# Turning bias vectors on TensorE, earlier residual rows and an earlier flip of h in a two-layer graph transformer

## The chip, the cores and the metric

The kernel runs on one core of a Trainium2 chip. The metric is the device time in microseconds of one execution; the time of a kernel is the median over its runs. A profile is taken of one further execution, and its instructions are what the views below are made of. The engines are called PE (TensorE, matmuls and transposes), DVE (VectorE), ACT (ScalarE), POOL (GpSimd) and SP (SyncE, which here only issues DMAs). Each runs its own instructions in the order in which the program emitted them.

## The reference

Two identical layers of a transformer over a graph of N = 2708 nodes with 512 features, 8 heads of 64, and a hidden width of 2048. All is float32.

```
mask = adj + eye
q, k, v = (h @ Wq.T + bq), (h @ Wk.T + bk), (h @ Wv.T + bv)     # 8 heads of 64
scores = q k^T / 8, set to -1e9 where mask == 0
ctx  = softmax(scores) @ v
h1   = layer_norm(h + ctx @ Wo.T + bo) * ln1_g + ln1_b
out  = layer_norm(h1 + relu(h1 @ W1.T + b1) @ W2.T + b2) * ln2_g + ln2_b
```

`adj` is a sparse symmetric 0/1 matrix; the kernel keeps lists of fewer than 24 neighbours a node.

## The kernel before

The nodes are worked on in 22 tiles of 128 (the last one holds 20). Because the graph is sparse, attention is done by edges: for each tile the rows of K and V of the listed neighbours are gathered from a table in DRAM (`kv_d`) and weighed on DVE and ACT. The schedule is written out by hand: the order of instructions in the program is their order on each engine.

**Stage one, keys and lists (`first`, L871).** For each of the 22 tiles, PE projects k and v (`project`, L575), ACT copies them out, POOL adds the bias row bk (L917), and ACT's queue stores the rows in `kv_d`. Beside it, `lists(t)` reads two halves of 128 rows of `adj` (SP, L691), POOL adds the diagonal (L694), ACT codes them (L700), and DVE finds the neighbours by MAX8 (L705). `counted` and `ranked` then sort the nodes by their number of neighbours; two matmuls (L788, L795) use the result.

**Stage two, queries (`first_queries`, L944).** 22 more projections; DVE evicts each with its bias (`evicted`, L951; the last, short tile also needs L597), SP stores pairs of tiles in `q_d` (`written`, L960 and L964). After the third, `last_keys` finishes `kv_d` and attention may begin. The tiles of attention come in the order of `blocks` (L1522), which begins with tiles of few neighbours. The first three tiles of attention make their own queries (`own_rows`, `turned_own`, `own_query`); all others gather theirs from `q_d` once all queries are stored (`asked`, L1073). `beside_queries(t)` is called after each query: it loads weights, settles biases (`settle`, L1276), and calls `advance`.

**Attention runs ahead by credit.** `attend` (L1527) is a generator of chunks of at most two neighbours. `advance(more)` (L1584) adds to a credit of at most 1.5 and emits chunks while it is positive; a chunk of two costs 1, of one 0.5, an empty step 0.2. `through(k)` (L1594) emits whatever is missing for a block. A finished tile leaves its context `cx` in `got`.

**Feed-forward, per block of two tiles.** `attended` (L1366) transposes cx on PE (`flip`, L1233, the tile `tp`), fetches the residual rows (`residuals`, L1357; in layer 0 a gather on POOL, in layer 1 a load on SP), projects by Wo (`o`), adds, and normalizes to h (`norm`, L1218, with the power of -1/2 on POOL, L1227). `turned` (L1389) flips h to hT. `feed_forward` (L1398) does 16 steps f: four matmuls into `pf` per step and pass (L1445), ACT's relu to `ft` (L1456), and the second matmul into `a` (L1418) three steps later. The main loop (L1635) places, after each step f of block k, what else is done there: the next block's residuals, flips and projection, chunks of attention by the tables `PACES` (block 0) and `PACE`, and in layer 0 the next layer's keys and values (`keys_values`, L1485).

**Biases.** `lined` (L560) copies bk and bq, which lie in DRAM as 128 x 4 columns, into a DRAM row by one DMA whose pieces are single elements; `row_of` (L567) reads this row into all partitions. `column` (L603) reads bv, b2 and the next layer's bo, which lie in DRAM as rows, into 128 x 4 columns, again element by element. `settle` negates b2 and bo and adds pairs of rows.

Of the kernel before, what the change touches and what calls it, by code (L numbers as in the profile page):

```python
# [479 lines left out]
def by_edges(ctx: ExitStack, tc: tile.TileContext, x, xT, adj, layers, out, redo):  # L480
# [35 lines left out]
    lines = []  # L516
# [43 lines left out]
    def lined(w, name, by):  # L560

        line = dram.tile([1, DM], F32, name=f"{name}_d{len(lines)}")
        lines.append(line)
        by.dma_start(out=line.rearrange("o (c p) -> p (o c)", p=P), in_=w[name])
        return line
# [37 lines left out]
    def column(w, name):  # L603
        t = small.tile([P, NC], F32, tag=name, name=name, bufs=1)
        nc.sync.dma_start(out=t, in_=w[name].rearrange("o (c p) -> p (o c)", p=P))
        return t
# [264 lines left out]
    def first(w, meanwhile):  # L871
# [29 lines left out]
        short = [lined(w, name, nc.scalar) for name in ("bk", "bq")]  # L901
        finish(halves)
        wv = matrix(w, "Wv", "wv")
        bk = row_of(short[0], "bk")
# [3 lines left out]
        for t in range(NT):  # L908
            r = size(t)
            if t == NT - 1:  # L910
                parts = placing[0](*counts)
            xs = tokens(t, 0)
            kv = wts.tile([P, 2 * DM], F32, tag=f"w2_{5 + t % 3}", name="kvs")
            k = project(xs, r, wk, "k")
            if t < NT - 1:
                nc.scalar.copy(kv[:r, :DM], k[:r])
                nc.gpsimd.tensor_tensor(kv[:r, :DM], kv[:r, :DM], bk[:r], ALU.add)  # L917
            v = project(xs, r, wv, "v", other=True)
            nc.scalar.copy(kv[:r, DM:], v[:r])
            if before:  # L920
                nc.scalar.dma_start(**before)
            before = dict(out=kv_d[0][t * P : t * P + r, :], in_=kv[:r])
            if t == 0:
                finish(load())
            while done < min(NT, 1 + LEAD * t):
                lists(done)
                done += 1
                if done == NT:
                    counts = counted()
            meanwhile(t)  # L930
            if t == QT:
                wq = matrix(w, "Wq", "wq", nc.gpsimd)
            if t == NT - 4:
                bq = row_of(short[1], "bq", DK**-0.5)
# [9 lines left out]
    def first_queries(bq, wq, parts, inverted, pa, tokens, last_keys, meanwhile):  # L944
# [21 lines left out]
        for t in range(NT):  # L966
# [25 lines left out]
            if t == OWN:  # L992
                zTs = [turned_own(g, xr) for g, xr in zip(blocks[0], xrs)]
                for g, zT in zip(blocks[0], zTs):
                    own_query(g, zT, to[g], bq, wq)
                    advance(0.5)
            if t == OWN + 5:
                own_query(order[2], turned_own(order[2], xrs[2]), to[order[2]], bq, wq)
# [247 lines left out]
    class Layer:  # L1246
# [5 lines left out]
        def load_first(self):  # L1252
            w = self.w
            self.wo = matrix(w, "Wo", "wo", nc.gpsimd if self.n == 0 else None)
            self.bv = column(w, "bv")
            if self.n == 0:
                self.bo = row(w, "bo")
            self.g1 = row(w, "ln1_g")
            self.nb2 = column(w, "b2")
            self.unsettled = [self.nb2]  # L1260
# [15 lines left out]
        def settle(self):  # L1276
            for t in self.unsettled:
                if isinstance(t, tuple):
                    nc.vector.tensor_tensor(t[0], t[0], t[1], ALU.add)
                else:  # L1280
                    nc.vector.tensor_scalar(t, t, -1.0, None, ALU.mult)
# [21 lines left out]
        def load_next(self):  # L1303

            nxt = layers[self.n + 1]
            self.short = [lined(nxt, name, nc.sync) for name in ("bk", "bq")]
            self.nbo = column(nxt, "bo")
            self.unsettled.append(self.nbo)

        def preloaded(self, tiles, temp):  # L1310
# [10 lines left out]
            return list(zip(tiles, places))  # L1321

# [250 lines left out]
    def settled():  # L1573

        held = small.tile([P, 1], F32, tag="held", name="held", bufs=1)
        nc.vector.tensor_reduce(held, flags, AX.X, ALU.min)
        pr = ps.tile([P, DM], F32, tag="g", name="pr")
        nc.tensor.matmul(pr[:1, :1], ones[:, :1], held, start=True, stop=True)
        nc.vector.tensor_scalar(redo, pr[:1, :1], P - 0.5, None, ALU.is_lt)
        return nc.values_load(redo[0:1, 0:1], min_val=0, max_val=1)  # L1580
# [29 lines left out]
    def beside_queries(t):  # L1610
# [9 lines left out]
        if t > OWN:  # L1620
            advance(0.65)
        if t == NT - 6:
            through(0)
            early[0] = now.attended(blocks[0], got)
            next(early[0])
        if t == NT - 5:
            for _ in blocks[0]:
                next(early[0])

# [5 lines left out]
    for n in range(NL):  # L1635
        last = n == NL - 1
        nxt = None if last else Layer(n + 1, layers[n + 1])
        if n > 0:
# [6 lines left out]
            both = dn.tile([P, 2, NC, P], F32, tag="hT", name="zTs", bufs=1)  # L1645
            for i, g in enumerate(order[8:10]):
                nc.sync.dma_start(out=both[:, i], in_=zT_d[n][g])
                pool.append((g, both[:, i]))
# [6 lines left out]
            for i, _ in enumerate(streamed):  # L1655
                if i == 4:
                    now.stores = nc.sync
                if len(got) < 2 or i < 4:
# [4 lines left out]
            streamed = now.queries(order[16 : 2 * AHEAD])  # L1663
            next(streamed)
            for _ in blocks[0]:
                next(early[n])
            for i, _ in enumerate(streamed):
                if i < 3:
                    advance(0.6)
            now.apart = False  # L1670
            now.load_w2(NFC // 2 - 1)
        *_, hs = early[n]
        hT = now.turned(blocks[0], hs)
        projecting = xbs = None
        for k, block in enumerate(blocks):
# [4 lines left out]
            for f, zs in enumerate(now.feed_forward(block, hs, hT)):  # L1680
# [24 lines left out]
                if last and not more and f == 8:  # L1705
                    checked()
                if last and not more and f == 14:
                    again = settled()
                if not more and f == 0:
                    finish(ahead)  # L1710
                if not last:
# [6 lines left out]
                    if (k, f) == (1, 0):  # L1718
                        now.settle()
                    if (k, f) == (NB - 1, 0):  # L1720
                        places.clear()
                        now.wq = matrix(nxt.w, "Wq", "wq")
                    if (k, f) == (1, 0):
                        now.bk = row_of(now.short[0], "bk")
                        nxt.bq = row_of(now.short[1], "bq", DK**-0.5)
# [83 lines left out]
```

## Time and profile before

| | |
|---|---|
| runs | 1880.89, 1882.51, 1883.33 us; median 1882.51 |
| profiled execution | 1880.68 us, of which the span from first to last instruction is 1879.0 us |
| mean granted clock of PE | 0.993 |
| busy | PE 1833.0 us, DVE 1373.1, ACT 944.1, POOL 781.8 |
| DMA | 368.00 MB, mean 196 GB/s |

Busy time is an instruction's own time; a line of the timeline gives the start, the duration, the engine, the program's line, the operation, out<-in with shapes, how many were merged, and in brackets the idle time of the engine before it with the instruction that ended it. "issue" there means that nothing the profile shows was waited for. The list of waits gives for an engine and line what it waited for: total microseconds, times, the longest. A row of the windows gives from:to, length, busy time and instructions of PE, weight loads, DVE, ACT and POOL, then the granted clock, the busy share of the DMA engines and the rate in GB/s. A name such as `L585` is a line of the kernel; all projections share that line.

### The profile page before, as it was taken

How to read it: one execution, taken by the hardware profiler on the slowest of the kernel's cores; microseconds unless marked ns; L12 is line 12 of the kernel's file. 1: busy time of each engine (PE TensorE's matmuls, PEld its weight loads, DVE VectorE, ACT ScalarE, POOL GpSimd, SP SyncE). 2: the span in 40 equal slices, each digit the busy share in tenths (PEclk: the TensorE clock that was granted, in tenths of full speed). 3: DMA queues.
4: the chain of work that ended last, by engine and by line, in shares of the span. 5: the costliest groups of instructions: out<-in, count | busy, mean ns of one | idle time of the engine just before them, and what ended most of it. 6: DMA issues, size and time to landing. Idle time of an engine off the chain costs nothing.

```text
span 1879.0 us, 20852 instructions
## 1 busy us (share of the span) xinstructions
PE 1833.0 (98%) x6140; PEld 1087.8 (58%) x6140; DVE 1373.1 (73%) x2143; ACT 944.1 (50%) x3261; POOL 781.8 (42%) x745
## 2 busy tenths in 40 slices
PE   7999978999999999999999999999999999999997
PEld 3444435656656566565665544566666666666664
DVE  3987847876867777677774237878988998899842
ACT  3771426555545555555553214556746575657531
POOL 3233745544444444353530113526543554455302
PEclk9999998999999999999999999999999999999999
DMA  9998958555465554554531477736545664545300
GB/s 279 367 340 258 379 182 308 185 174 173 153 212 174 185 184 141 196 192 137 191 124 69 144 256 291 288 133 217 220 157 196 215 236 140 216 169 203 128 1 20
DMA packets 133933, 368.00 MB, mean 196 GB/s; under 512 B 18518, under 2 KB 36774, under 8 KB 133808
## 3 DMA queue, kind: packets, MB, share of 16 engines
q0 software_dynamic: 70608, 252.12, 38.7%
q1 hardware_dynamic: 53106, 93.63, 14.5%
q10 hardware_dynamic: 10094, 20.81, 3.0%
q8 instruction: 50, 0.82, 0.2%
q14 instruction: 75, 0.61, 0.1%
HBM read 315.84 MB, written 50.68 MB: 195 GB/s over the span
## 4 chain that ended last, share of the span: by engine, by line
PE 88%; DVE 4%; DMA 4%; issue 2%; ACT 1%; POOL 1%; ACTq 0%; POOLq 0%; SPq 0%; DVEq 0%
PE pf L1445 29%; PE a L1418 29%; PE v L585 8%; PE k L585 8%; PE o L585 7%; PE q L585 4%; PE tp L1237 2%; DVE kv L1101 1%; DMA kv<-kv_d,listed 1%; DVE sc L1107 1%; DMA bq_d<-in_bq 1%; DMA q_d<-qs 1%; ACT kv L1127 1%; PE a L1433 1%; DMA xb<-in_x,ident_i 0%
## 5 line engine op out<-in xcount | busy, mean ns | idle before, releaser
L1445 PE MATMUL pf<-hT,w 128*128 128x256 f32 (+1 forms) x2816 | 634.7, 373 | 18.7 <-ACT ft L1456 15.6
L1445 PEld LDWEIGHTS pf<-hT,w 128*128 128x128 f32 x2816 | 520.0, 191 | 192.9 <-issue 104.3
L1418 PE MATMUL a<-w,ft 128*128 128x512 f32 x1312 | 611.1, 592 | 0.0
L1064 POOL DMA_INDIRECT kv<-kv_d,listed x420 | 502.2, 1196 | 256.5 <-issue 113.1
L1456 ACT ACTIVATE ft<-pf,b 128x256 f32<-128x256 f32 (+1 forms) x336 | 154.3, 462 | 415.4 <-PE pf L1445 411.6
L1418 PEld LDWEIGHTS a<-w,ft 128*128 128x128 f32 x1312 | 246.9, 190 | 187.5 <-issue 166.6
L1227 POOL TENSOR_TENSOR rd<-va,mhalf 128x1 f32<-128x1 f32 (+1 forms) x88 | 81.8, 929 | 584.7 <-DVE va L1225 584.7
L1127 ACT ACTIVATE kv<-kv,p 128x64 f32<-128x64 f32 x1232 | 311.0, 334 | 5.0
L1101 DVE TENSOR_TENSOR kv<-kv,q 128x1024 f32<-128x1024 f32 (+1 forms) x222 | 256.9, 1157 | 21.5 <-DMA q<-q_d,ident_i 15.7
L1107 DVE TENSOR_REDUCE sc<-kv 128x16 f32<-128x1024 f32 (+1 forms) x222 | 258.0, 1162 | 7.6
L1140 DVE TENSOR_TENSOR acc<-acc,kv 128x1024 f32<-128x1024 f32 (+2 forms) x178 | 205.4, 1154 | 78.4 <-ACT kv L1127 66.8
L1120 ACT ACTIVATE p<-sc,listed 128x8 f32<-128x8 f32 x420 | 104.7, 300 | 144.6 <-DVE sc L1107 103.8
L1133 DVE TENSOR_TENSOR kv<-kv,p 128x512 f32<-128x512 f32 (+1 forms) x178 | 122.6, 689 | 47.0 <-ACT p L1120 28.6
L585 PE MATMUL o<-wo,cT 128*128 128x512 f32 x336 | 149.6, 598 | 0.0
L585 PEld LDWEIGHTS o<-wo,cT 128*128 128x128 f32 x336 | 64.2, 192 | 81.6 <-issue 76.2
L705 DVE MAX8 tops<-code 128x8 f32<-128x247 f32 (+2 forms) x242 | 78.5, 400 | 35.9 <-ACT code L700 35.9
L1231 DVE SCALAR_TENSOR_TENSOR h<-h,rd,ln_b 128x512 f32<-128x512 f32 (+1 forms) x88 | 66.5, 755 | 39.9 <-POOL rd L1227 39.9
L1171 ACT ACTIVATE cx<-acc,su 128x64 f32<-128x64 f32 (+1 forms) x352 | 88.2, 333 | 13.4 <-DVE su L1163 7.7
L1380 DVE TENSOR_TENSOR h<-o,xb 128x512 f32<-128x512 f32 (+1 forms) x44 | 30.2, 687 | 86.7 <-PE o L585 53.2
L1127 ACT ACTIVATE acc<-kv,p 128x64 f32<-128x64 f32 (+1 forms) x352 | 88.9, 335 | 1.4
L585 PE MATMUL k<-wk,xg 128*128 128x512 f32 x168 | 77.4, 604 | 11.6 <-DMA wk<-in_Wk 11.6
L700 ACT ACTIVATE code<-aj 128x1354 bf16<-128x1354 int32 (+1 forms) x44 | 72.8, 1720 | 19.0 <-POOL aj L694 13.8
(168 smaller groups left out, 1522.7 us busy)
## 6 DMA issues: line engine op xcount, KB each, us to landing
aj<-in_adj SPq DMA_DIRECT2D x42, 677.0 KB
kv_d<-kvs ACTq DMA_DIRECT2D x21, 512.0 KB
xg<-in_xT SPq DMA_DIRECT2D x19, 512.0 KB
w<-in_W SPq DMA_DIRECT2D x16, 512.0 KB
kv<-kv_d,listed POOLq DMA_INDIRECT x420
zT_d<-zT SPq DMA_DIRECT2D x22, 256.0 KB
xb_d<-h SPq DMA_DIRECT2D x21, 256.0 KB
q<-q_d SPq DMA_DIRECT2D x21, 256.0 KB
```

Of the source, the lines that this page charges most:

```text
L585: nc.tensor.matmul(o[:r], xs(c), wm[:, c, :], start=(c == 0), stop=(c == NC - 1))
L1064: return nc.gpsimd.indirect_dma_start(out=to, out_offset=None, in_=table[:, :], in_offset=bass.IndirectOffsetOnAxis(ap=s, axis=0), bounds_ ...
L1101: nc.vector.tensor_tensor(kv[:r, :c, :DM], kv[:r, :c, :DM], self.q[:r].unsqueeze(1).to_broadcast([r, c, DM]), ALU.mult,)
L1107: nc.vector.tensor_reduce(self.sc[:r, s0 : s0 + c, :], kv[:r, :c, :DM].rearrange("p s (h d) -> p s h d", d=DK), AX.X, ALU.add,)
L1120: nc.scalar.activation(p[:r, s, :], self.sc[:r, s, :], AF.Exp, bias=minus[:r, g, s : s + 1])
L1127: nc.scalar.activation(to[:, i, hd], kv[:r, i, DM + h * DK : DM + (h + 1) * DK], AF.Copy, scale=p[:r, s0 + i, h : h + 1],)
L1133: nc.vector.tensor_tensor(to[:, 0, :].rearrange("p (h d) -> p h d", d=DK), kv[:r, 0, DM:].rearrange("p (h d) -> p h d", d=DK), p[:r, s0, : ...
L1140: nc.vector.tensor_tensor(self.acc[:r, :c, :], self.acc[:r, :c, :], kv[:r, :c, DM:], ALU.add)
L1171: nc.scalar.activation(cx[:r, hd], self.acc[:r, 0, hd], AF.Copy, scale=self.su[:r, h : h + 1])
L1418: nc.tensor.matmul(a[:r], fts[f][:, c0 : c0 + r], self.w2[f // 2][:, f % 2, :], start=(f == 0), stop=(f == NFC - 1),)
L1445: nc.tensor.matmul(pf[:, :w], self.w1[f // 2][:, c, f % 2 * P : f % 2 * P + P], hT[:, c, :w], start=(c == 0), stop=(c == NC - 1),)
L1456: nc.scalar.activation(ft[:, :w], pf[:, :w], AF.Relu, bias=self.b1[:, f : f + 1])
```

## The change

Three things are changed together.

1. *Biases.* bk and bq are loaded as 128 x 4 columns (`given_columns`, SP), transposed on PE into one PSUM tile, copied by ACT, and stored as two DRAM rows of 4 x 128 (`lined`). In layer 0 this stands behind k of tile 0, and tile 0's bias is added at the end of its turn. bv, b2 and bo are loaded as 4 x 128 rows (`raw_columns`), and `settle` transposes them on PE and takes the sign on DVE. The next layer's bk and bq are loaded in `load_next`, turned at (k, f) = (1, 0) and read back at (1, 2).
2. *Residual rows and attention in layer 0.* The first block's own queries come one query later than their flips (`OWN + 1`), and `advance` starts one query later; the residual rows are gathered at query NT - 10 instead of NT - 6, the flips of cx come at NT - 7, the projection by Wo at NT - 6.
3. *h before the last query.* In both layers h of the first block is turned in front of the last query instead of behind it. In layer 1 two queries are loaded in advance (`two`), one stands between the flips of cx and the projection by Wo, and one `advance(0.6)` is gone.

Further, `settled` is split in two, so that its DVE reduction is emitted at step 11 and the rest at step 14.

```
-        short = [lined(w, name, nc.scalar) for name in ("bk", "bq")]
+            if c == 0:
+                cols = given_columns(w)
...
-        bk = row_of(short[0], "bk")
...
             k = project(xs, r, wk, "k")
             if t < NT - 1:
                 nc.scalar.copy(kv[:r, :DM], k[:r])
+            if t == 0:
+                short = lined(cols, nc.scalar)
+            elif t < NT - 1:
                 nc.gpsimd.tensor_tensor(kv[:r, :DM], kv[:r, :DM], bk[:r], ALU.add)
...
+            if t == 0:
+                bk = row_of(short[0], "bk")
+                nc.gpsimd.tensor_tensor(kv[:r, :DM], kv[:r, :DM], bk[:r], ALU.add)
             meanwhile(t)

+    def lined(cols, by):
+        pr = ps.tile([P, DM], F32, tag="g", name="pr")
+        short = dn.tile([P, DM], F32, tag="row", name="short", bufs=3)
+        for i, col in enumerate(cols):
+            nc.tensor.transpose(pr[:NC, i * P : (i + 1) * P], col, ident)
+        nc.scalar.copy(short[:NC, : 2 * P], pr[:NC, : 2 * P])
+        lines = []
+        for i in range(2):
+            line = dram.tile([NC, P], F32, name=f"line{len(all_lines)}")
+            all_lines.append(line)
+            by.dma_start(out=line, in_=short[:NC, i * P : (i + 1) * P])
+            lines.append(line.rearrange("(o c) p -> o (c p)", o=1))
...
+                to, raw, sign = t
+                pr = ps.tile([P, DM], F32, tag="g", name="pr")
+                nc.tensor.transpose(pr[:, :NC], raw, ident[:NC, :NC])
+                nc.vector.tensor_scalar(to, pr[:, :NC], sign, None, ALU.mult)

-        if t > OWN:
+        if t > OWN + 1:
             advance(0.65)
+        if t == NT - 10:
+            early[0] = now.residuals(blocks[0])
+        if t == NT - 7:
+            through(0)
+            early[0] = now.attended(blocks[0], got, early[0])
+            next(early[0])
         if t == NT - 6:
-            through(0)
-            early[0] = now.attended(blocks[0], got)
-            next(early[0])
-        if t == NT - 5:
             for _ in blocks[0]:
                 next(early[0])
+        if t == NT - 2:
+            *_, early[0] = early[0]
+            early[0] = early[0], now.turned(blocks[0], early[0])

             next(early[n])
-            streamed = now.queries(order[16 : 2 * AHEAD])
-            next(streamed)
+            now.query(order[16], both[:, 0])
             for _ in blocks[0]:
                 next(early[n])
-            for i, _ in enumerate(streamed):
-                if i < 3:
-                    advance(0.6)
+            streamed = now.queries(order[18 : 2 * AHEAD])
+            next(streamed)
+            now.query(order[17], both[:, 1])
+            advance(0.6)
+            next(streamed)
+            advance(0.6)
+            *_, hs = early[n]
+            early[n] = hs, now.turned(blocks[0], hs)
+            finish(streamed)
...
                     if (k, f) == (1, 0):
                         now.settle()
+                        short = lined(now.cols, nc.sync)
...
-                    if (k, f) == (1, 0):
-                        now.bk = row_of(now.short[0], "bk")
-                        nxt.bq = row_of(now.short[1], "bq", DK**-0.5)
+                    if (k, f) == (1, 2):
+                        now.bk = row_of(short[0], "bk")
+                        nxt.bq = row_of(short[1], "bq", DK**-0.5)
```

## Prediction

> **What bounds the kernel now.** I read the page first, then the list of waits of TensorE (PE), then the timeline and the rows of short windows at the places that this list names.
>
> ```profile
> PE 1833.0 (98%) x6140; PEld 1087.8 (58%) x6140; DVE 1373.1 (73%) x2143; ACT 944.1 (50%) x3261; POOL 781.8 (42%) x745
> ...
> PE pf L1445 <- ACT ft L1456: 15.6, 1, 15.6
> PE k L585 <- DMA wk<-in_Wk: 11.6, 1, 11.6
> PE tp L1237 <- DVE qs L951: 2.2, 1, 2.2
> ```
>
> PE is busy 98% of 1879.0 us, so only its 46 us of idle time and stretched matmuls can be won. Two places hold most of it: 11.6 us at the start and one stall of 15.6 us early in layer 0. The start in short windows (from:to, length, five engines, clock, DMA share, GB/s) and SP's waits there:
>
> ```profile
> 5.00:6.00 1.00, 0.00 (x0) 0.00 (x0) 0.00 (x0) 0.00 (x0) 1.00 (x1) 1.00 1.79 119
> 6.00:7.00 1.00, 0.00 (x0) 0.00 (x0) 0.00 (x0) 0.00 (x0) 1.00 (x1) 1.00 0.84 14
> ...
> 11.00:12.00 1.00, 0.43 (x1) 0.46 (x2) 0.00 (x0) 0.00 (x0) 0.00 (x0) 1.00 0.88 277
> ...
> SPq L552 <- DMA bk_d<-in_bk: 7.5, 1, 7.5
> SPq L552 <- DMA bq_d<-in_bq: 2.4, 1, 2.4
> ...
> 21.09 3.60 PE L585 MATMUL k<-wk,xg 128*128 128x512 f32 x8
> ```
>
> The engines are "busy" and move next to nothing while bk and bq are turned by 4-byte stores into DRAM (1024 pieces); SP's next loads wait for them. Keys of tile 1 start only at 21.09; tile 0's work is 2 x 3.43 us, so 14.2 us are lost. The stall, in the timeline:
>
> ```profile
> 250.70 0.69 DVE L1380 TENSOR_TENSOR h<-o,xb 128x512 f32<-128x512 f32 x1 [10.00 <-DMA xb<-in_x,ident_i]
> ...
> 260.12 0.66 PE L1237 MATMUL tp<-ident,h 128*128 128x128 f32 x4 [2.21 <-DVE qs L951]
> 261.23 5.29 PE L1445 MATMUL pf<-hT,w 128*128 128x256 f32 x16 [0.46 <-ACT hT L1242]
> ...
> 265.13 2.13 DVE L597 SCALAR_TENSOR_TENSOR qs<-q,qs 20x512 f32<-20x512 f32 x3
> 267.63 0.68 SPq L564 DMA_DIRECT2D bk_d<-in_bk  x1
> ...
> 282.90 1.23 DVE L1101 TENSOR_TENSOR kv<-kv,q 128x1024 f32<-128x1024 f32 x1 [15.65 <-DMA q<-q_d,ident_i]
> ...
> 288.38 3.63 PE L1445 MATMUL pf<-hT,w 128*128 128x256 f32 x8 [15.63 <-ACT ft L1456]
> ```
>
> Read upwards: PE waits for an ACT activation that stands behind the fourth tile's attention; that waits for its q rows, which can be gathered only when the last queries are stored. The last query's eviction (L597) ended at 267.26 because VectorE (DVE) stood 10.00 us waiting for residual rows; the chain of waits has the stores landing at 277.48, 10.2 us after that, with layer 1's 4-byte turns of bk, bq and bo right behind them on SP's queue.
>
> **The change, part by part.** The sum is made against the profiled execution, 1880.68 us; the median of the three runs is 1.83 us higher.
>
> *Start.* Removed: both 4-byte turns on ACT's queue. Added on SP after the first piece of Wk: two loads of 128 pieces of 16 bytes; two transposes behind k of tile 0, one ACT copy (an eviction of 512 columns takes 0.58, so under 0.6), two stores of four 512-byte rows on ACT's queue. Before tile 1 the DMA must bring 2.5 MB (x, Wk, Wv). Traffic begins at about 2.2 us. At 375 GB/s (the rows from 20 to 120 us lie at 364 to 398, one at 333) that is 6.7 us, at some 270 (the mean of the six rows from 15 to 21 us, where loads start up again) 9.3 us; with 0.5 for the small pieces and 0.9 for the last two matmuls, tile 1 starts at 10.3 to 12.9 instead of 21.09: 8.2 to 10.8 won. The second half of the stage, the lists (aj, then DVE's MAX8), must shift too: DVE ends "before" at 158.55 and PE uses it at 158.87, so PE has 0.3 us of slack. The first aj landed at 26.38; 4.4 MB stand up to it, 11.7 to 16.3 us, landing at 14.4 to 19.0: 7.4 to 12.0 won. I take **-9.0**, ends -2 (a late bk row, below) and -11.
>
> [...] The nearest row is bv and b2 of layer 1, also small pieces into SBUF: 1024 of them, issued at 1064.51 and 1065.97, with the rate at 395, 402, 279, 160 and 374 GB/s in windows of 2 us: some 620 KB missed, 1.7 us. So 256 pieces cost about 0.4; I use 0.5.
>
> *Layer 0, queries.* Own queries, attention's credit and `settle` move one query later; the first kv rows land at 192.37 anyway, so nothing is lost there. Following the credits through the code, the steps up to the fourth tile are the same, each one query later, and cx of the second tile is ready at about 230.5 where PE wants it at 230.2; half of the flips come before it, so I charge nothing (if DVE is later, 1 to 2 us). The residual gathers (two, 1.3 us each on POOL) go in front of list and kv gathers that are wanted much later; POOL's own pow for h, though, stands behind its backlog until about 242 and costs h about 1 us. DVE's work from the query after the flips (234.7): five evictions of 0.7, chunks of 2.45, 2.45 and 1.37, weighing 4.5, two h of 4.4, POOL's 1.0, the last eviction 2.77: about 26.8, ending at 261.5 instead of 267.26: -5.8. The last store then has only small SBUF loads behind it. Its cost is bounded by the store of the last keys, a like tile of 20 rows (179.27 to 182.17, 2.90), and by today's 10.2; nearest is the 2.90: -7.3. From there on gather (5.4), chunk (2.45), ACT (2.9) stay as they are. Together **-13.1**, ends -6 and -15. A stall of some 8 us remains, with its slow restart (3.63 for 8 matmuls that take 1.89 later).
>
> The gap of 2.21 before the flip of h goes, since the last query (1.06) follows h; hT's evictions (1.14 each) are mostly under it. That win lies in front of the stall and is eaten by it. [...]
>
> *Layer 1, first block.* The last query now covers hT: -1.05 (PE's wait at 1190.19). One `advance(0.6)` fewer, and o comes one query later; by the credits cx of the fourth tile is then made by the forced `through` at f=10 instead of at f=9. DVE is gapless from 1196 to 1230 and that cx ends at 1229.16 while PE flips it at 1227.64, so this is the next thing that is late: weighing waits for one more activation, 1.5 us. Net **+0.4**, ends -1.2 and +4. Later blocks meet the same order again. The wait for the second cx (1163) stays.
>
> *The rest.* Nine small transposes at 0.11 (eight of a flip take 0.87): **+1.0**. The split of `settled` moves a reduction that had long ended (DVE idle 10.69 before the next): 0. Bias columns on SP at (0, 9) and in `load_first`, the rows read at (1, 2): wanted at f=5 at the earliest, 10 us later; 0, and if PE caught up, the wait for one landing, some 3 us. POOL's scaling of bq is only moved.
>
> Sum: -9.0 - 13.1 + 0.4 + 1.0 = **-20.7**: 1860.0 for such an execution, 1861.8 for a median, rounded to 1862.
>
> **The rivals.**
> *The bias row comes late.* In tile 0 SP waits at `row_of` for a chain over PE, ACT and DRAM, with the next aj loads behind it, and POOL's bias add stands in front of the next diagonal add. I reckon the row at 19 us, in time. Today's round trip was 10.5 and the row 6.4; with these and a line issued at 10.7 it lands at 27.6, list 1 is ready at 31.5 when DVE has been free since 23.5, and 8 of the 9 us are gone: 1870. For: SP has one queue. Against: the new stores are 2 KB in eight pieces, and the old slowness was that of 1024.
> *The stores were not slow through the pieces behind them.* Then the 7.3 us stay: 1869. For: they are queued ahead of the pieces. Against: the rate falls to 13 and then 0 GB/s from 270 to 278, with nothing else in flight.
> *Slower than before.* The same SP wait, but lasting: past about 19 us each further us of the bk row holds aj loads, POOL's diagonal add and the lists one for one, and PE meets them at 158.87. It costs 1 us per us and turns the change slower once the row lands after some 42 us: at 50 us 1890. Nothing in the trace is that slow.
> [...]
>
> **How the numbers follow.** Forecast 0.70 (1856 to 1867, with the 1865 case in it), late row 0.12, slow stores 0.08, both together 0.02 (1877), slower 0.06, no change 0.02. The range 1855 to 1873 holds the first three but for their edges. This kernel's runs can tell about 0.2% (4 us) from nothing. Faster 0.92, same 0.02, slower 0.06.
>
> **What would show it.** After: keys of tile 1 start at 10.3 to 12.9 us; no wait of SP for bk_d; DVE's first wait for code ends near 19 instead of 28; no 10 us wait for xb; PE's wait for ft near 8 us; the flip of h without a wait; a wait of 1 to 2.5 us for cx at f=10 of layer 1's first block. I am wrong if tile 1 still starts after 18 us, if PE waits over 2 us at L795, or if the wait for ft stays above 12 us.

## The result, and the profile after

The changed kernel takes 1866.6 us in the median of four runs (1862.9 to 1867.7), the kernel before 1882.6 beside it; the ratio is 0.991, with a 95% interval of 0.990 to 0.993. Timed once more on another occasion (`after_again` below) it was 0.992 (0.991 to 0.994). The forecast was 1862 in a range of 1855 to 1873: faster, as said, and inside the range, but less fast than the sum of the parts. That sum was 20.7 us for a profiled execution; the two profiled spans differ by 14.6 (1879.0 and 1864.4). Where the 6.1 us went is the question of this part.

First the engines' row of the profile's page and TensorE's (PE's) waits over 1 us, in total, times, longest:

```profile
PE 1833.7 (98%) x6149; PEld 1088.4 (58%) x6149; DVE 1373.0 (74%) x2145; ACT 944.3 (51%) x3263; POOL 778.2 (42%) x745
```

```profile
PE pf L1488 <- ACT ft L1499: 9.1, 1, 9.1
PE k L602 <- DMA wk<-in_Wk: 4.6, 1, 4.6
PE tp L1268 <- ACT cx L1202: 2.9, 4, 1.3
PE q L597 <- DMA zT<-zT_d: 2.7, 1, 2.7
```

PE's busy time is what it was; the span less it is 30.7 us instead of 46. The two large waits of before have shrunk: the one for ft, in the stall of layer 0 ("the ft wait" from here on), from 15.6 to 9.1, and the one for Wk at the start from 11.6 to 4.6. The flip of h has no large wait left. The wait for cx has grown from 1.2 to 2.9, and the last line is new: a query of layer 1 waits for its turned tile zT. (The lines have moved: L585 is now L602, L1445 is L1488, L1456 is L1499, L597 is L614, L1101 is L1132, L1237 is L1268.)

The start, in windows of 1 us, in SP's waits, and in the timeline:

```profile
5.00:6.00 1.00, 1.00 (x2) 0.10 (x1) 0.00 (x0) 0.00 (x0) 1.00 (x1) 1.00 0.96 326
6.00:7.00 1.00, 1.00 (x2) 0.62 (x2) 0.00 (x0) 0.00 (x0) 1.00 (x1) 1.00 1.00 334
```

```profile
SPq L587 <- DMA line<-short: 5.5, 1, 5.5
```

```profile
4.63 6.04 PE L602 MATMUL k<-wk,xg 128*128 128x512 f32 x8 [4.63 <-DMA wk<-in_Wk]
...
14.16 3.60 PE L602 MATMUL k<-wk,xg 128*128 128x512 f32 x8
...
18.64 3.58 DVE L727 MAX8 tops<-code 128x8 f32<-128x247 f32 x11 [17.70 <-ACT code L722]
...
21.33 1.27 POOL L957 TENSOR_TENSOR kvs<-kvs,bk 128x512 f32<-128x512 f32 x1 [4.51 <-DMA bk<-line]
```

The DMAs move 326 and 334 GB/s where they moved 119 and 14, SP no longer waits for a turned bias before its next weights, and the keys of tile 1 start at 14.16 instead of 21.09: 6.9 us won, though later than the forecast's 10.3 to 12.9. Tile 0's keys take 6.04 us, tile 1's 3.60. (SP still waits 5.5 us for the turned row itself, at L587.)

The end of the queries and the stall of layer 0, in the timeline:

```profile
248.56 1.04 PE L1268 MATMUL tp<-ident,h 128*128 128x128 f32 x8
250.65 7.17 PE L1488 MATMUL pf<-hT,w 128*128 128x256 f32 x32
253.50 2.13 DVE L614 SCALAR_TENSOR_TENSOR qs<-q,qs 20x512 f32<-20x512 f32 x3
259.67 1.01 POOL L1095 DMA_INDIRECT q<-q_d,ident_i  x1 [2.58 <-DMA bq<-in_bq]
263.19 1.23 DVE L1132 TENSOR_TENSOR kv<-kv,q 128x1024 f32<-128x1024 f32 x1 [7.56 <-DMA q<-q_d,ident_i]
265.70 0.49 ACT L1151 ACTIVATE p<-sc,listed 128x8 f32<-128x8 f32 x2 [12.36 <-DVE sc L1138]
268.66 3.74 PE L1488 MATMUL pf<-hT,w 128*128 128x256 f32 x8 [9.12 <-ACT ft L1499]
```

The flip of h no longer waits, and the last eviction (L614) ends at 255.6 instead of 267.26. The rows q are gathered 4.0 us after that instead of 11.2. PE resumes at 268.66 instead of 288.38. The chain itself is as before: PE waits for a relu (L1499) that stands on ACT behind an exponential (L1151) of the fourth tile, which waits for DVE, which waits for q.

Last the head of layer 1, in the timeline of before, then in the timeline and in windows of 2 us after:

```profile
1162.56 0.60 PE L1237 MATMUL tp<-ident,cx 128*128 128x128 f32 x4
...
1182.16 7.18 SPq L1354 DMA_DIRECT2D q_d<-qs  x3
...
1189.94 0.91 SPq L1329 DMA_DIRECT2D zT<-zT_d  x2
...
1190.19 7.17 PE L1445 MATMUL pf<-hT,w 128*128 128x256 f32 x32 [1.05 <-ACT hT L1242]
...
1253.46 1.04 PE L1237 MATMUL tp<-ident,h 128*128 128x128 f32 x8
```

```profile
1144.10 0.60 PE L1268 MATMUL tp<-ident,cx 128*128 128x128 f32 x4
...
1162.53 7.73 SPq L1397 DMA_DIRECT2D q_d<-qs  x3
...
1169.02 7.07 PE L1488 MATMUL pf<-hT,w 128*128 128x256 f32 x32
1170.83 0.97 SPq L1372 DMA_DIRECT2D zT<-zT_d  x2
1180.48 1.92 PE L597 MATMUL q<-wq,zT 128*20 128x512 f32 x8 [2.67 <-DMA zT<-zT_d]
...
1210.57 0.60 PE L1268 MATMUL tp<-ident,cx 128*128 128x128 f32 x4
1212.48 0.33 PE L1268 MATMUL tp<-ident,cx 128*128 128x128 f32 x1 [1.32 <-ACT cx L1202]
...
1239.86 1.04 PE L1268 MATMUL tp<-ident,h 128*128 128x128 f32 x8
```

```profile
1178.00:1180.00 2.00, 0.00 (x0) 0.00 (x0) 1.90 (x4) 0.92 (x4) 1.31 (x2) 1.00 1.08 390
1180.00:1182.00 2.00, 1.52 (x8) 0.16 (x8) 1.97 (x3) 0.00 (x0) 1.65 (x1) 0.54 0.98 308
```

SP spends 7.73 us on three stores, because the last waits for the eviction of the query that now stands directly in front of the feed-forward block; the loads of zT behind it leave at 1170.83, 1.8 us after the block has begun (before: 1189.94, 0.25 us ahead of it), into DMAs that are full (share 1.01 to 1.08, 390 to 416 GB/s from 1170 to 1180). PE waits 2.67 us for them and comes back at a clock of 0.54. SP stood nearly as long at these stores before (7.18 us). What is new is that the flip of h and the wait for hT no longer lie between the last query and the block, so that the block starts some 2 us earlier against the loads. Thirty us after the wait for zT, PE waits for the fourth tile's context.

The shift against the profile before, point by point; "this part" is what came since the row above, and the forecast's step stands beside it:

| from the profile's start to | after less before | this part | forecast |
|---|---|---|---|
| tile 1's keys | -6.93 | -6.9 | -9.0 |
| first ranking matmul (151.49) | -6.94 | 0.0 | 0 |
| PE's return from the ft wait | -19.72 | -12.8 | -13.1 |
| first context of layer 1 (1144.10) | -18.46 | +1.3 | +1.0 |
| flip of h for layer 1's second block | -13.60 | +4.9 | +0.4 |
| end | -14.6 | -1.0 | 0 |

### The profile page after: what moved, and what is told of

The parts are those of the page before. It is cut to its first block, busy times and chain, and to the rows that moved or that the text cites. A ratio compares the mean times of both kernels' runs of the same rounds, so it can differ in the third digit from the quotient of the medians.

```text
span 1864.4 us, 20896 instructions
## 1 busy us (share of the span) xinstructions
PE 1833.7 (98%) x6149; PEld 1088.4 (58%) x6149; DVE 1373.0 (74%) x2145; ACT 944.3 (51%) x3263; POOL 778.2 (42%) x745
## 4 chain that ended last, share of the span: by engine, by line
PE 92%; DVE 3%; DMA 2%; issue 2%; ACT 1%; POOL 0%; ACTq 0%; SPq 0%; POOLq 0%; DVEq 0%
PE pf L1488 31%; PE a L1461 31%; PE k L602 8%; PE v L602 8%; PE o L602 7%; PE q L602 4%; PE tp L1268 3%; PE a L1476 1%; DMA kv<-kv_d,listed 1%; DMA zT<-zT_d 1%; DVE kv L1132 0%; DVE sc L1138 0%; DMA q_d<-qs 0%; ACT kv L1158 0%; ACT cx L1202 0%
## 5 line engine op out<-in xcount | busy, mean ns | idle before, releaser
L1488 PE MATMUL pf<-hT,w 128*128 128x256 f32 (+1 forms) x2816 | 635.2, 373 | 10.0 <-ACT ft L1499 9.1
L1488 PEld LDWEIGHTS pf<-hT,w 128*128 128x128 f32 x2816 | 520.1, 191 | 185.1 <-issue 107.3
L1499 ACT ACTIVATE ft<-pf,b 128x256 f32<-128x256 f32 (+1 forms) x336 | 153.8, 461 | 432.9 <-PE pf L1488 427.9
L1132 DVE TENSOR_TENSOR kv<-kv,q 128x1024 f32<-128x1024 f32 (+1 forms) x222 | 257.1, 1158 | 10.6 <-DMA q<-q_d,ident_i 7.6
L1138 DVE TENSOR_REDUCE sc<-kv 128x16 f32<-128x1024 f32 (+1 forms) x222 | 258.0, 1162 | 7.6
L1151 ACT ACTIVATE p<-sc,listed 128x8 f32<-128x8 f32 x420 | 104.7, 300 | 143.9 <-DVE sc L1138 114.5
L602 PE MATMUL o<-wo,cT 128*128 128x512 f32 x336 | 148.0, 593 | 0.0
L602 PEld LDWEIGHTS o<-wo,cT 128*128 128x128 f32 x336 | 63.7, 190 | 81.1 <-issue 76.6
L602 PE MATMUL k<-wk,xg 128*128 128x512 f32 x168 | 78.0, 608 | 4.6 <-DMA wk<-in_Wk 4.6
```

The source lines that it names most:

```text
L602: nc.tensor.matmul(o[:r], xs(c), wm[:, c, :], start=(c == 0), stop=(c == NC - 1))
L1132: nc.vector.tensor_tensor(kv[:r, :c, :DM], kv[:r, :c, :DM], self.q[:r].unsqueeze(1).to_broadcast([r, c, DM]), ALU.mult,)
L1138: nc.vector.tensor_reduce(self.sc[:r, s0 : s0 + c, :], kv[:r, :c, :DM].rearrange("p s (h d) -> p s h d", d=DK), AX.X, ALU.add,)
L1151: nc.scalar.activation(p[:r, s, :], self.sc[:r, s, :], AF.Exp, bias=minus[:r, g, s : s + 1])
L1488: nc.tensor.matmul(pf[:, :w], self.w1[f // 2][:, c, f % 2 * P : f % 2 * P + P], hT[:, c, :w], start=(c == 0), stop=(c == NC - 1),)
L1499: nc.scalar.activation(ft[:, :w], pf[:, :w], AF.Relu, bias=self.b1[:, f : f + 1])
```

## The experiments

The theory to be tested had three parts: the start is carried whole to the end; the stall of layer 0 shrank through the earlier rows and through the 4-byte pieces that no longer follow the last store; the new order of layer 1 costs more than it wins. Each kernel below was timed beside the kernel before, on four occasions, on which the medians of before were 1882.6, 1878.6, 1880.0 and 1879.7, so that ratios are compared, and spans of the profiles where a part of the span is meant. The interval of a ratio is some 3 us to either side. The medians alone therefore do not tell the four variants of layer 1 below, or `warm_start`, from the changed kernel (0.991 and 0.992); what these edits do is read from the stages of the profiles, where the same instructions agree within 0.2 us when nothing disturbs them (in layer 1, from PE's return behind the second context to the end of Wo's projection, 11.9 us in six of them).

**The start alone** (`start_only`), made from the kernel before:

```
+            if c == 0:
+                cols = given_columns(w)
...
-        short = [lined(w, name, nc.scalar) for name in ("bk", "bq")]
-        bk = row_of(short[0], "bk")
...
+            if t == 0:
+                short = turned_lines(cols, nc.scalar)
```

> The kernel before with the start of the change alone: the two bias columns loaded as they lie, turned on TensorE behind tile 0's keys, the row read at tile 0; every later line as before. Theory: the start is carried one to one to the end, since nothing between tile 1 and the first feed-forward block is bound by anything but TensorE: tile 1's keys at 14.2 instead of 21.1, the ft wait still about 15.6 us, the span shorter by the 6.9 us that the changed kernel showed here (1872 to 1873 of 1879). Rival: work of DVE, GpSimd and the DMAs that did not start earlier (the lists, the weights) takes a part back at the next wait, and less than 4 us reach the end, with the ft wait longer by the rest.

Measured: 1874.9 us, a ratio of 0.998 (0.997 to 0.999), so 3.7 us less; the profiled run's span is 1872.7, so 6.3 less than the profile before. The median is with the rival, the profile's span with the theory. The timeline shows that the span agrees by luck, and that the path is the rival's:

```profile
13.96 3.60 PE L610 MATMUL k<-wk,xg 128*128 128x512 f32 x8
...
154.12 0.71 PE L820 MATMUL pr<-before,ones 128*128 128x264 f32 x2 [2.22 <-DVE before L792]
```

Tile 1 is 7.1 us earlier, but at the ranking matmuls PE waits 2.2 us for DVE's lists, and 4.7 us of the gain are left. The stall, with its 4-byte pieces, was only 11.2 us in this profile, 4.4 less than in the one before, though nothing there was changed. So the start is worth between 4 and 7 us at the end: the lists have no slack to spare. In the changed kernel's profile this wait was zero. Why the lists were 2 us later here was not settled; between 60 and 152 us ACT waited 11.0 us for POOL's diagonal adds and 3.0 for pieces of `adj`, where it waited 3.4 and 1.4 in the changed kernel's profile. A wait of over 2 us at this place was one of the prediction's signs of being wrong.

**The 4-byte pieces back behind the last store** (`next_elements`):

```
-            self.cols = given_columns(nxt)
+            self.short = [lined_bits(nxt, name, nc.sync) for name in ("bk", "bq")]
...
-                        short = lined(now.cols, nc.sync)
```

> The changed kernel, with layer 1's bk and bq turned by 4-byte pieces from DRAM to DRAM on SP's queue again, as before, and the two rows read from there; all else as changed. Theory: those pieces, issued right behind the last query's store, are what made that store and the gather of q slow; the ft wait goes from 9.1 back to about 16 us, the clock comes back slowly as before, and the span is 6 to 8 us longer (1870.5 to 1872.5 against 1864.4). Rival (named with the prediction): the store was slow for another reason, such as the gathers' and weights' traffic; the ft wait stays within 1.5 us of 9.1 and the span within 1.5 us.

Measured: 1869.5 us, a ratio of 0.995 (0.993 to 0.997); span of the profiled run 1872.2. The timeline, and two windows of the wait:

```profile
269.94 1.23 DVE L1140 TENSOR_TENSOR kv<-kv,q 128x1024 f32<-128x1024 f32 x1 [15.00 <-DMA q<-q_d,ident_i]
...
275.41 3.78 PE L1496 MATMUL pf<-hT,w 128*128 128x256 f32 x8 [14.42 <-ACT ft L1507]
```

```profile
260.00:262.00 2.00, 0.99 (x3) 0.16 (x1) 0.00 (x0) 0.00 (x0) 1.01 (x1) 1.00 0.50 19
264.00:266.00 2.00, 0.00 (x0) 0.00 (x0) 0.00 (x0) 0.00 (x0) 0.50 (x1) 0.50 0.75 68
```

DVE's wait for q doubles (7.56 to 15.00), the ft wait is 14.4 again, and the rate falls to 19 GB/s while the DMA engines are half busy (share 0.50): the theory holds, and the rival named with the prediction (the stores slow for another reason) falls. The size is not steady, though. The profiled run is the longest of the four; the spans of the other three are 1866.9 to 1867.8, 2.5 to 3.4 us over the changed kernel's profile, and by the ratios it is 5 to 7 us. With pieces DVE's wait for q was 15.65, 11.24 and 15.00 in three profiles; without them it was 7.4 to 8.1 in the nine that have the same chunk at the head of the block.

**The residual rows gathered late** (`late_xb`): the two lines at query NT - 10 are gone, and `attended` fetches the rows at NT - 7.

> The changed kernel without the early gather of the residual rows: they are gathered where layer 0's context tiles are turned (seven queries ahead of the end instead of ten), so behind three more queries' lists and keys on GpSimd's queue; h is still turned in front of the last query. Theory of the prediction: the early gather brought the last eviction forward by some 6 us; without it DVE waits for xb, its in-order evictions hold TensorE, and the span is 3 to 6 us longer (1867.5 to 1870.5). Rival: in the changed kernel the rows landed some 10 us ahead of their use (issued at 218.6 and 220.6, used at 231.8), so that most of it was slack: DVE waits under 2 us, and the span stays within 1 us of 1864.4.

Measured: 1870.0 us, a ratio of 0.995 (0.994 to 0.997), span 1867.9. The timeline has the wait back:

```profile
237.13 0.69 DVE L1423 TENSOR_TENSOR h<-o,xb 128x512 f32<-128x512 f32 x1 [4.76 <-DMA xb<-in_x,ident_i]
```

The gathers now leave at 229.1 and 230.5 and DVE stands 4.8 us; the first feed-forward block starts at 253.70 instead of 250.65. The early gather is worth 3.05 us in this stage (3.5 in the spans, 5 to 7 by the ratios), as the theory had it at its low end.

**h turned behind the last query in layer 0** (`h_behind`):

```
-            early[0] = early[0], now.turned(blocks[0], early[0])
...
+        if n == 0:
+            early[0] = early[0], now.turned(blocks[0], early[0])
```

> The changed kernel, with layer 0's h turned behind the last query again instead of in front of it (layer 1 keeps the new order). Theory of the prediction: turning h first hides the hT wait and the gap of 2.2 us behind the last evictions, and without it the first feed-forward block starts 0.5 to 1.5 us later and the span is as much longer. Rival: the end of this stage is set by the last query's eviction, store and gather; the last query now runs 1 us earlier, so the stall ends that much earlier and TensorE's later start is absorbed: TensorE resumes behind the stall 0 to 1 us earlier, and the span is the same or up to 1 us shorter.

Measured: 1865.7 us, a ratio of 0.993 (0.992 to 0.995) where the changed kernel beside it has 0.992; spans 1862.5 and 1863.0.

```profile
252.08 7.17 PE L1488 MATMUL pf<-hT,w 128*128 128x256 f32 x32 [1.06 <-issue]
...
266.65 3.39 PE L1488 MATMUL pf<-hT,w 128*128 128x256 f32 x8 [5.69 <-ACT ft L1499]
```

The block starts 1.7 us later (250.37 in `after_again`) and PE still returns from the stall 0.3 us earlier (266.95 there): the ft wait is 5.7 instead of 7.7. The medians cannot be told apart. The rival holds, and it is what the prediction itself said of this win. A gain in front of a stall that something else ends is worth nothing here.

**Layer 1's old order** (`l1_old`), all else as changed:

```
-            now.query(order[16], both[:, 0])
+            streamed = now.queries(order[16 : 2 * AHEAD])
+            next(streamed)
...
-                if len(got) < 2 or i < 3:
+                if len(got) < 2 or i < 4:
```

> The changed kernel, with layer 1's order around its first block as before: tiles 16 to 20 streamed as one row of queries, h turned after the last of them, four and three advances of the attention instead of three and two; start and layer 0 as changed. Theory: the new order of layer 1 lost 3.9 us (the loads of zT behind the last query's store, and the fourth tile's context a step later), more than the 1 us wait for hT that it removed; the span is 3 to 4.5 us shorter than the changed kernel's (1860 to 1861.5 against 1864.4), with the hT wait of about 1 us back and no wait for zT. Rival: the 3.9 us come from elsewhere (the earlier start shifts the attention's phase against the feed-forward blocks), the order itself gains the hT wait, and the span is 0 to 2 us longer.

Measured: 1859.8 us, a ratio of 0.990 (0.988 to 0.992), span 1860.7, that is 3.7 less than the changed kernel. From the first context of layer 1 to the flip of h for its second block it takes 91.1 us, the kernel before 90.9, the changed one 95.8. No wait for zT is left, and the wait for hT (1.05) is back. The theory holds in the stage. The next two kernels take its two halves apart.

**The last stores from ACT's queue** (`store_act`):

```
+            now.stores = nc.scalar
             finish(streamed)
+            now.stores = nc.sync
```

> The changed kernel, with the stores of layer 1's queries 18 and 19 (the last two in front of its first feed-forward block) issued from ACT's queue instead of SP's; nothing else moves. Theory: in the changed kernel SP waits 7.7 us for the eviction of the last query before it can issue that store, and the loads of zT of the streamed block stand behind it in SP's queue; from ACT's queue the store holds up no load, zT lands before it is used, the 2.7 us wait of TensorE for zT and the slow clock after it go, and the layer 1 part from the first feed-forward block to the fourth tile's context (41.6 us in the changed kernel) falls to about 37.5. Span 3 to 4.5 us shorter with the same ft wait (some 1860.5). Rival: the loads land late because the DMAs are saturated in that stretch (their share there is about 1.0), whatever issues them: the wait for zT stays over 1.5 us and the part over 40 us.

Measured: 1862.2 us, a ratio of 0.991 (0.989 to 0.992); span 1857.6.

```profile
1162.48 1.80 SPq L1372 DMA_DIRECT2D zT<-zT_d  x2
...
1168.07 7.07 PE L1488 MATMUL pf<-hT,w 128*128 128x256 f32 x32
...
1205.42 0.60 PE L1268 MATMUL tp<-ident,cx 128*128 128x128 f32 x4
```

zT now leaves 5.6 us before the block begins instead of 1.8 after it, and from the block to the fourth tile's flip PE takes 37.35 us instead of 41.55: 4.2 us, of which 2.67 were the wait and the rest the slow clock behind it (0.54 and 0.60 in the changed kernel's two windows from 1180 to 1184, 1.00 after). The rival is right that the DMAs are full from 1168 us on (share 0.90 to 1.06, 336 to 426 GB/s up to 1178); but they move nothing from 1160 to 1162 (0 GB/s), and a load issued at 1162.5 is in time.

**A third advance in front of the block** (`third_advance`): one line, `advance(0.6)`, behind the two that are there.

> The changed kernel with a third advance of the attention in front of layer 1's first feed-forward block, as before had: one line more. Theory: the fourth tile's context was finished a step later because the credit of that advance was missing, and was forced at the moment it was needed; with it TensorE's waits for cx in layer 1's first block (1.3 and twice 0.15 us) and the slow clock behind them go: some 2.5 to 3.5 us less, with the wait for zT unchanged at about 2.7 (span about 1861.5 at the same ft wait). Rival: the context is late because DVE and GpSimd are behind in that stretch, not by the order; the step more only delays the last queries' evictions, and the wait for cx stays over 1 us with a span within 1 us or longer.

Measured: 1863.2 us, a ratio of 0.991 (0.990 to 0.993); span 1861.9.

```profile
1182.80 1.05 PE L597 MATMUL q<-wq,zT 128*20 128x512 f32 x8 [3.61 <-DMA zT<-zT_d]
...
1211.43 1.04 PE L1268 MATMUL tp<-ident,cx 128*128 128x128 f32 x8
```

The flip of the fourth tile takes 1.04 us without a wait, the wait for zT stays (3.6), and from this flip to the second block's h it takes 25.0 us instead of 29.3; the span is 2.5 less. The theory holds in place, and in size by the span; the medians do not show it. Of the 4.3 us, 1.2 are lost ahead of this flip (the wait for zT is longer, and behind the wait for the second context PE took 13.55 us to the end of Wo's projection instead of 11.90), and 1.0 behind the second block's h: in the profiles with the late context (this kernel's parent, `store_act`, `h_behind`) the remainder of the program takes 624.5 us, in those without it (`l1_old`, `third_advance`, `l1_mended`, and before) 625.5. The reason is not known.

**Both together** (`l1_mended`):

> The changed kernel, with layer 1's new order kept and its two costs removed: the stores of queries 18 and 19 from ACT's queue, and the third advance. Theory: the two are independent (4.2 us of the zT loads, 2.5 to 4 us of the late context), and the new order is then worth what it was meant for, the hT wait: 6 to 8 us less than the changed kernel, a span of 1856.5 to 1858.5, and 2 to 4 us less than with layer 1's old order (1860.7). Rival: the two share a cause (one late stretch of DMA or DVE); together they bring no more than the better one alone, and the span is 1860 or more.

Measured: 1860.2 us, a ratio of 0.9895 (0.988 to 0.991), beside 0.992 for the changed kernel; span 1859.3. The spans and stages here are compared with `after_again`. From the first block to the second block's h it takes 63.2 us instead of 71.0: 4.4 us less up to the fourth tile's flip and 3.5 less behind it (`store_act` alone 65.0, `third_advance` alone 66.0). So the two do add up in their places, to 7.8 us. At the end only 3.7 are left in the profile and 4.9 in the median, less than the 6 to 8 expected. In this profile the wait of 1.57 us for the second context was followed by a clock of 0.50 (the window from 1148 to 1150), and the stretch up to the first block took 26.6 us instead of 24.9: 1.8 lost. Another 1.1 is given back in the remainder as said, and 1.2 lies ahead of layer 1, where nothing was changed. So the new order, with both costs removed, is no measurable gain over the old one (0.9895 and 0.990).

**Work for PE while it waits for Wk** (`warm_start`):

```
+        pr = ps.tile([P, DM], F32, tag="g", name="warm")
+        for _ in range(8):
+            nc.tensor.matmul(pr[:, :P], ident, ident, start=True, stop=True)
```

> The changed kernel with eight 128x128 matmuls of the identity with itself, into a PSUM tile that nobody reads, ahead of tile 0's keys, while TensorE waits for Wk (1.4 to 4.6 us); all else as changed. Theory: tile 0's keys take 6.0 to 6.8 us where the next tile's take 3.6, since TensorE works at half pace after standing idle (its 512-column steps come every 0.85 us instead of 0.43) although the clock row shows 1.00; kept busy beforehand it runs at full pace from its first loaded piece, tile 0's keys end 1.3 to 2 us earlier, and with them tile 1 (12.2 to 12.9 instead of 14.2). Rival: the pace is that of the pieces of Wk and of the tokens, which land one by one while the DMAs move all they can; tile 0's keys end within 0.4 us of 10.7, and tile 1 within 0.4 of 14.2.

Measured: 1864.7 us, a ratio of 0.991 (0.990 to 0.993).

```profile
5.00 4.30 PE L602 MATMUL k<-wk,xg 128*128 128x512 f32 x8
...
10.01 3.70 PE L602 MATMUL v<-wv,xg 128*128 128x512 f32 x8 [0.50 <-DMA wv<-in_Wv]
13.55 1.88 PE L602 MATMUL k<-wk,xg 128*128 128x512 f32 x4
```

Tile 0's keys take 4.30 us instead of 6.04, with the same loads, and end at 9.3 instead of 10.7: as the theory had it. Tile 1 starts only 0.6 us earlier, at 13.55 where the theory had 12.2 to 12.9, since v then waits for Wv; at the end nothing can be told from no change. Both are true of this stage, one behind the other: PE at half pace first, the DMAs next.

**The left-over credit held back** (`hold_credit`):

```
+            if (n, k) == (0, 0):
+                credit = min(credit, 0.0)
             for f, zs in enumerate(now.feed_forward(block, hs, hT)):
```

> The changed kernel, with the attention's credit left over from the queries (1.15) set to zero in front of layer 0's first feed-forward block, so that the first chunk of the fourth tile is not emitted at step 0 of that block but at step 4; one line. Theory: the ft wait that is left (7.2 to 9.1 us) is one of order: ACT's queue holds that chunk's exponential, which needs q from DRAM, in front of the block's next activations; emitted later, q has landed before ACT comes to it, the ft wait falls under 2 us and the slow clock after it goes: 7 to 10 us less (a span of 1854 to 1858). Rival: TensorE is only the first to stand still: the fourth tile's context is then forced at step 12 where the second block's context is turned, and TensorE waits there for nearly as long; the span is within 3 us of the changed kernel's.

Measured: 1857.6 us, a ratio of 0.988 (0.986 to 0.989); span 1855.5.

```profile
260.14 1.89 PE L1488 MATMUL pf<-hT,w 128*128 128x256 f32 x8
...
265.44 1.23 DVE L1132 TENSOR_TENSOR kv<-kv,q 128x1024 f32<-128x1024 f32 x1 [11.18 <-DMA q<-q_d,ident_i]
265.57 0.47 ACT L1499 ACTIVATE ft<-pf,b 128x256 f32<-128x256 f32 x1 [2.78 <-PE pf L1488]
...
267.95 0.49 ACT L1151 ACTIVATE p<-sc,listed 128x8 f32<-128x8 f32 x2 [1.90 <-DVE sc L1138]
```

DVE still waits 11.18 us for q, longer than the 7.56 in the changed kernel, and PE no longer notices: its wait for ft is gone, since the relus now stand in front of the fourth tile's exponential (267.95) on ACT; the last of them, at 265.57, is done before it. The context forced at step 12 is there without a wait. The theory holds: 8.9 us less in the spans where the wait was 9.1, and 7 to 9 by the ratios. The changed kernel's stall is thereby shown to be one of order on ACT, not of how fast q comes. The stall of before has the same chain in the prediction's lines, but this edit was not tried there.

**The changed kernel again** (`after_again`) and **all four edits together** (`all_mended`):

> The changed kernel once more, unaltered, on the chip and beside the runs on which the next three are timed. Every theory: the ratio of the first measurement, 0.991, and the same waits; the ft wait, which was 7.2 to 9.1 us in the kernels that share this stage, says how much of a difference between single profiles is scatter.

> The changed kernel with all four edits: the credit set to zero in front of layer 0's first feed-forward block, the two stores from ACT's queue, the third advance, and eight matmuls of the identity while TensorE waits for Wk. Theory: they act at four places on TensorE's path and add up: 9 + 4.2 + 3 + 0.6, some 17 us less than the changed kernel (a span of 1846 to 1849; a ratio to the kernel before of about 0.982). Rival: with the stall gone DVE, at 74% busy, or the DMAs become what TensorE waits for in layer 1's first block, and half of the layer 1 gain is lost (a span of 1851 or more).

Measured beside each other: 1865.0 us, 0.992 (0.991 to 0.994), span 1863.0, ft wait 7.7; and 1849.4 us, 0.984 (0.983 to 0.986), span 1845.6. The four edits bring 15.6 us in the median and 17.4 in the spans. PE's waits over 0.5 us in the second:

```profile
PE warm L928 <- POOL ident masks.py:199: 1.4, 1, 1.4
PE tp L1271 <- ACT cx L1205: 1.1, 2, 0.9
PE pf L1491 <- ACT fts L1502: 0.8, 1, 0.8
PE tp L1271 <- DVE h L1265: 0.6, 1, 0.6
```

Some 17 us were expected. No other large wait took the place of what was removed. This is the fastest kernel here.

## Why the prediction was right, and where it was off

**The start: -9.0 forecast, -6.9 seen, and between -4 and -7 at the end.** The cause was read rightly: the rate at 14 GB/s was the 4-byte pieces, and without them it is over 320 in the same windows. `next_elements` puts some 3 to 8 us on 1024 such pieces from DRAM to DRAM in the way of a store. What the 256 pieces of 16 bytes cost, no run shows, neither the 0.5 taken for them nor the price of the 4-byte pieces in the 1865 case, which was the author's estimate; the DMAs moved 207, 334 and 210 GB/s in the three windows from 2 us on (188, 154 and 193 before), and PE did not stand still between 4.63 and tile 1. The mis-sized term is "0.9 for the last two matmuls". The forecast let tile 0's work run under the loads. In the profile k of tile 0 begins at 4.6 us, when its first piece of Wk has landed; then 6.0 of keys, 0.1 of transposes and 3.4 of values follow one after the other: 14.2. Of that, 1.7 (6.04 less the 4.30 of `warm_start`) is half pace: tile 0's keys have four steps of 0.85 us, where tile 1's take 0.43 each. `warm_start` shows that it can be removed, and the windows' clock column shows 1.00 all the while.

**The late bias row did not happen.** It landed at 21.3 us, 2.3 later than reckoned, and SP did wait 5.5 us for it at `row_of`; DVE's first wait ended at 18.6, as forecast ("near 19"). The case of a slower kernel needed some 42 us.

**Layer 0's queries: -13.1 forecast, -12.8 seen.** The last eviction came 4.7 us earlier beside the start (5.8 forecast), and the gap from there to the gather fell by 7.1 (7.3 forecast). The way from the gather to PE's return, which the forecast left as it was, became 1.0 us shorter. So the terms are right in kind, but that the sum is met within 0.3 is luck: 1.1 too much and 1.0 left out cancel. In the six other profiles that share this stage the part is -14.0 to -14.7, inside the forecast's ends. The wait of PE that is left is 9.1 (forecast 8; 7.2 to 9.1 in these profiles). The experiments confirm two of the terms, the rows with 3 us and the pieces with 3 to 8, and the statement that the early flip of h is eaten by the stall. What the rest of the 4.7 is, some 2 us, was not tested: the flips of cx and Wo's projection also came one query earlier.

**Layer 1: +0.4 forecast, +4.9 in this stage and +3.9 at the end.** This is the step that failed. The 1.05 us for hT were right: from the first context to the block it is 24.6 to 25.2 us in the profiles with the new order in which the clock stays up, 26.5 to 26.9 in those in which it falls, and 27.6 and 27.8 in the kernel before and in `l1_old`, where it fell too (Wo's projection took 8.62 us in `l1_old`, 7.03 in the changed kernel). That the clock fell in the profile of before (0.50 in the window from 1166 to 1168) and not in the changed kernel's (1.00 from 1143 to 1152) is luck of some 1.7 us; without it the stage would have cost 6.6 (an estimate, 4.9 and 1.7). "cx of the fourth tile is then made by the forced `through`" was right too, but 1.5 us was the wait alone; with the slow clock behind it (0.58 and 0.57 in the windows from 1214 to 1218) it cost 3.5, of which 1.0 came back. What was missing altogether is SP's queue: the text follows the last query past hT and DVE, and not past the store that it brings and the loads of zT behind that store. That is the 4.2 us of `store_act`. The ends given for this term (-1.2 and +4) did not reach the +4.9 that the stage cost.

**The rest, +1.0, was +1.3.** In sum the forecast span was 6 us too short: 2.1 from the start, 0.3 and 0.3 from the two middle parts, 3.5 from layer 1.

## What to carry to other kernels

Where one instruction is moved in front of a stage, follow every queue it is moved past: here a store that waited for one eviction held up two loads behind it, and that cost 4.2 us where the move won 1.05. Before speeding up what a stalled engine waits for, ask whose order makes it wait: one line that kept an exponential out of the relus' way was worth 9 us, more than the whole new start. And a gain in front of a stall that something else ended was worth nothing here: in `h_behind` the block began 1.7 us later and PE was back from the stall 0.3 us earlier.

## What the runs showed of the hardware

The clock after a short gap was not a matter of the gap's length alone. In the same place, from PE's return behind its wait for layer 1's second context to the end of Wo's projection, it took 13.60, 13.55, 13.55 and 13.29 us in the profiles of `hold_credit`, `third_advance`, `warm_start` and `l1_mended` (waits of 1.15, 1.29, 1.52 and 1.57 us) and 11.9 in those of the changed kernel, `after_again`, `h_behind`, `store_act` and `next_elements` (1.24, 1.18, 1.36, 1.38 and 1.48). In `l1_mended`, where PE resumed at 1146.05, the clock in the windows of 2 us from 1146 on reads 0.73, 0.50 and 0.92; in the changed kernel's profile it reads 1.00 from 1143 to 1152. What is missing to 1.00 adds up to 1.7, which is 3.4 us at half. The falls are alike: 1.7 is also what is missing in the kernel before at this place (wait 1.05; PE resumed at 1164.21; 0.77, 0.50, 0.50 and 0.52 in the windows of 1 us from 1165 on), and in the changed kernel behind its waits for zT (0.54 and 0.60 in windows of 2 us from 1180) and for the fourth tile's context (0.58 and 0.57 from 1214). By these windows PE had been back at work for 0.9 us in `l1_mended` and 1.3 in the kernel before when the clock fell. Why it fell behind one of these gaps and not behind another of like length, no run here shows.

The other surprise is how much the 4-byte pieces vary: the stall behind them was 15.6, 14.4 and 11.2 us in the profiles of before, `next_elements` and `start_only`, while without them it was 7.2 to 9.1 in seven profiles with the same order.
